# Four-layer graph network: setup rows for the second half made in groups 2 to 4, and a new static order

## The chip, the core and the metric

The kernel runs on one core of a Trainium2 chip. The metric is the device time of one execution in microseconds; the time before is the median of three runs, and the change is judged by the median time of the changed kernel. One of the three runs before (4820.43 us) stands apart from the other two and takes no part in the reasoning.

## The reference

The input is x, 128 graphs of 64 nodes with 512 features in float32, and an adjacency matrix of 64x64 per graph. Four layers follow each other. Each takes `h = relu(layernorm(x))` and adds its result to x.

```
layer 0:  h1 = relu(D^-1 H B^-1 H^T (h W1^T) + b1);  y = D^-1 H B^-1 H^T (LN(h1) W2^T) + b2;  x += y + h
layer 1:  A = exp(lrelu(8 tanh((s_i + s_j)/8))) * adj, s = (h w) a;  x += rownorm(A) * rowsum(adj) @ h @ w
layer 2:  x += rownorm(adj * exp(q k^T)) @ v,  q, k, v linear in h
layer 3:  T = rownorm(adj * exp(lrelu(sj_j + si_i + ab)));  x += relu(sum over k = 0..2 of T^k h Wk[k] + bk[k])
          sj, si: products of (h Wv + bv) with the two halves of a vector aw
```

Three small quantities that depend on weights alone matter for the change. `gb` is Wk^T bq, needed by the logits of layer 2. `c3` is Wv times each half of aw, two rows of 512, and `kap` is the sum of bv with both halves of aw, plus ab; all of these are needed by layer 3.

## The kernel before

The 128 graphs are taken as 16 groups of four tiles of 128 rows, two graphs to a tile. A first half runs layers 0 and 1 over the groups and stores x to a scratch tensor `xm`. A second half loads it again and runs layers 2 and 3. The weights of the halves share memory, so the halves are apart. Every large product is written as seven half-size products instead of eight (`strassen`, `chained`, and `product` in layer 3, where it is nested), which costs TensorE a little less and gives VectorE the sums and differences.

No loop sets the order in which instructions stand. The Python code records operations in a graph, each with an engine, an estimated cost and a priority, and `Graph.run` plays a list scheduler over that graph and writes out one fixed order for each engine: TensorE (PE), VectorE (DVE), ScalarE (ACT), GpSimd (POOL) and SyncE (SP). On SP stands every DMA. An engine takes its list strictly from the top, and SP does too: a DMA that waits for a buffer to come free holds up all DMAs behind it. The priority of an operation is a running number `G.prio` plus a shift from the table `AT`, set by `part(name)`. `PERIOD1` and `PERIOD2` space the groups of the two halves, and `STRETCH` scales the advance inside each layer. So a changed number in these tables can reorder everything.

Where the scheduler leaves TensorE a gap of over 1 us and a PSUM bank is free, `fill` puts matmuls of `ones` with `ones` in. They compute nothing that is used. Each such matmul has two records in the profile, as all float32 matmuls here.

Buffers are the other constraint. `tmp` has four slots of 128x512 floats; they take weight rows that are loaded for setup (`temp`) and, in layer 0, the planes of each `transposed` step, eight per group. `o` has two slots.

Setup code that comes ahead of group 0 is, in this order: `setup_l2` (Wq^T Wk, stored to a scratch tensor), the combinations of W1 and W2, `setup_l0`, `setup_l1`, the combinations of w, and then `setup_bq` and `setup_l3`:

- `setup_bq` loads four blocks of Wk, forms their sum weighted by bq in four DVE operations, multiplies by a column of ones on PE, and copies the result to `gb`.
- `setup_l3` loads ab, then for each half of aw: the half, bv, and four blocks of Wv, with five dot products on DVE (`dot`), and `spread`, which turns a column into a row over all partitions (one DVE product, one PE matmul, one ACT copy).

`setup_w3`, called under `part("wp")` for groups 1 and up, prepares the factors of the layer 3 weights during the first half; its loads are placed after the key `("z", g, k)`, which names the last operation of the normalisation between the two convolutions of layer 0 in that group. Such a key is for the scheduler alone: the semaphores of the built program follow from the memory that instructions touch.

In layer 3, `part("b0")` begins the long run of weight products of a group (L1124), whose weights are streamed from scratch tensors `fac`.

Of the kernel before, what the change touches and what calls it, by code (L numbers as in the profile page):

```python
# [14 lines left out]
P = 128  # L15
C = 64
D = 512
DH = 1024
T = 4
KD = D // P  # L20
# [151 lines left out]
def tile_adj_preln_d4(  # L172
# [6 lines left out]
    nc = tc.nc  # L179
    NG = adj.shape[0]  # L180
    G = Graph()
# [31 lines left out]
    def size(shape):  # L213
        n = 1
        for d in shape[1:]:
            n *= d
        return n

    for two in TWO:
        both = work.tile([P, max(sum(size(shape) * n for _, shape, n in tags) for tags in two)], F32,  # L220
                         name="_".join(tag for tags in two for tag, _, _ in tags))
        for tags in two:
            at = 0
            for tag, shape, n in tags:
                for i in range(n):
                    v = both[:, at:at + size(shape)]
                    at += size(shape)
                    if len(shape) == 3:
                        v = v.rearrange("p (a b) -> p a b", a=shape[1])
                    elif len(shape) == 4:  # L230
                        v = v.rearrange("p (a b c) -> p a b c", a=shape[1], b=shape[2])
# [23 lines left out]
    def c_mm(n, count):  # L255
        return 2 * count * max(n * 2 / 2400 + 0.0025, 0.111)
# [6 lines left out]
    def pe(cost, fn, r, w):  # L263
        return G.op("PE", cost, fn, r, w)

    def dve(cost, fn, r, w):
        return G.op("DVE", cost, fn, r, w)

    def dvp(cost, fn, r, w):
        return G.op("DVE", cost, fn, r, w, port=1)  # L270

    def act(cost, fn, r, w):
        return G.op("ACT", cost, fn, r, w)
# [7 lines left out]
    def dma(kb, fn, r, w, issue=0.34, lat=2.0):  # L281
        return G.op("SP", max(kb / 380.0, issue), fn, r, w, lat)

    def quad(b):
        return b.t.rearrange("p (c k) -> p c k", c=4)
# [1 line left out]
    FILL, LAT = 0.5, 2.3  # L287


    STRETCH, PERIOD1, PERIOD2 = (2.4057, 23.1237, 14.6194, 5.0478), 88.385, 152.83  # L290
    AT = {
        "x0": -4649.81, "apart": 515.41, "w1": 891.32, "b1": 147.15, "w2": 1055.04, "w": 146.66, "c1": 74.0, "l0":
        181.27, "c2": 131.25, "l1": 1241.14, "c": -4314.2, "g0": -2118.58, "g1": -4213.04, "g2": -574.45, "g3":
        -1827.82, "g": -443.79, "bq": -420.39, "l3": -143.58, "wg": 627.97, "wp": 228.79, "beg0": -1054.79, "beg1":
        -138.73, "end00": 1.09, "end01": -86.62, "end11": 256.44, "new2": -124.9, "new3": 81.75, "end2": -68.63,
        "end3": -133.99, "load1": -63.98, "load2": 661.26, "m": -63.44, "h0": 2.91, "p0": 25.16, "z0": -386.05,
        "q0": 47.65, "y0": -4107.25, "h1": -19.07, "p1": 5.7, "z1": -84.16, "q1": 20.96, "y1": -130.14, "s": -234.6,
        "t0": -462.0, "e0": -467.09, "t1": -348.17, "e1": -282.93, "hT": 524.3, "sh": 245.53, "lq": 730.58, "pt":
        -113.04, "v": 589.88, "pv": 1100.8, "s3": 672.72, "tt": 1008.78, "a0": 690.15, "b0": 538.95, "a1": 811.73,
        "ws": 2002.18, "load3": 441.07, "bk": 299.55,  # L300
    }

    def part(name):
        G.shift = AT[name]
# [28 lines left out]
        dma(8, lambda: nc.sync.dma_start(sb, src), [], [name])  # L333
        return sb

    def load_tmp(tag, n, shape_of, src):
        b = Buf(tag)
        dma(n * P * 4 / 1024, lambda: nc.sync.dma_start(shape_of(b.t), src), [], [b])
        return b

    def temp(src):

        return load_tmp("tmp", D, lambda t: t, src)

    xt, adjs, xmid, rows = {}, {}, {}, []

    def load_group(g, src, apart=0.0):
        b = Buf("adj")
        dma(500, lambda: nc.sync.dma_start(b.t, adj[g]), [], [b])
        adjs[g] = b  # L350
        for t in range(T):
            xx = Buf("x")
            at, key = src(g, t)
            G.shift += apart
            dma(300 if src is x_mid else 256, lambda xx=xx, at=at: nc.sync.dma_start(xx.t, at), key, [xx], lat=LAT if src is x_mid else 2.0)
            xt[g, t] = xx
# [27 lines left out]
    c3_b = const.tile([P, 2, D], F32, name="c3_b")  # L384
# [5 lines left out]
    def dot(in0, in1, acc, r, w):  # L390
        j = Buf("o")
        dvp(0.77, lambda: nc.vector.scalar_tensor_tensor(j.t, in0(), 1.0, in1(), op0=ALU.mult, op1=ALU.mult,
                                                         accum_out=acc()), r, [*w, j])
# [61 lines left out]
    def spread(col, dst, r, key):  # L455

        dg, p = Buf("tmp"), Buf("ps")
        dvp(0.75, lambda: nc.vector.tensor_mul(quad(dg), ident[:, None, :].to_broadcast([P, KD, P]),
                                               col()[:, :, None].to_broadcast([P, KD, P])), r, [dg])
        pe(c_mm(512, 1), lambda: nc.tensor.matmul(p.t, ones, dg.t, start=True, stop=True), [dg], [p])  # L460
        act(0.6, lambda: nc.scalar.copy(dst(), p.t), [p], [key])

    def setup_l1():
        wa, a_b = Buf("col"), temp(a.partition_broadcast(P))
        for c in range(KD):
            dot(lambda c=c: w_sb[:, c, :], lambda: a_b.t, lambda c=c: wa.t[:, c:c + 1], [(wm, c // 2), (wm, "given"), a_b], [(wa, c)])
        spread(lambda: wa.t, lambda: wa_b.t, [(wa, c) for c in range(KD)], wa_b)
# [15 lines left out]
            act(0.6, lambda c=c, e=e: nc.scalar.copy(e.t, ps[c].t), [ps[c]], [e])  # L483
            dma(256, lambda c=c, e=e: nc.sync.dma_start(wg_d[c * P:(c + 1) * P, :], e.t), [e], ["wg_d"])

    def setup_bq():

        pg, bk = Buf("ps"), Buf("o")
        for o in range(KD):
            k_ = temp(Wk[o * P:(o + 1) * P, :])  # L490
            if o == 0:
                dvp(0.45, lambda k_=k_: nc.vector.tensor_scalar(bk.t, k_.t, bq_c[:, 0:1], None, op0=ALU.mult), [k_, "bq_c"], [bk])
            else:
                dvp(0.85, lambda o=o, k_=k_: nc.vector.scalar_tensor_tensor(bk.t, k_.t, bq_c[:, o:o + 1], bk.t, op0=ALU.mult, op1=ALU.add),
                    [k_, "bq_c", bk], [bk])

        def mg():
            for c in range(KD):
                nc.tensor.matmul(pg.t[:, c:c + 1], bk.t[:, c * P:(c + 1) * P], ones[:, 0:1], start=True, stop=True)
        pe(c_mm(1, KD), mg, [bk], [pg])  # L500
        dve(0.2, lambda: nc.vector.tensor_copy(gb_c, pg.t[:, :KD]), [pg], ["gb"])

    def setup_l3():
        kk = Buf("mv")
        ab_t = load_tmp("rs", 1, lambda t: t, ab.partition_broadcast(P))
        for s in range(2):
            av, cc = temp(aw[s * D:(s + 1) * D].partition_broadcast(P)), Buf("col")
            bv_t = temp(bv3.partition_broadcast(P))
            dot(lambda bv_t=bv_t: bv_t.t, lambda av=av: av.t, lambda s=s: kk.t[:, s:s + 1], [bv_t, av], [(kk, s)])
            for c in range(KD):  # L510
                wv = temp(Wv3[c * P:(c + 1) * P, :])
                dot(lambda wv=wv: wv.t, lambda av=av: av.t, lambda c=c, cc=cc: cc.t[:, c:c + 1], [wv, av], [(cc, c)])
            spread(lambda cc=cc: cc.t, lambda s=s: c3_b[:, s, :], [(cc, c) for c in range(KD)], ("c3", s))
        dve(0.15, lambda: nc.vector.tensor_add(kap, kk.t[:, 0:1], kk.t[:, 1:2]), [(kk, 0), (kk, 1)], ["kap"])
        dve(0.15, lambda: nc.vector.tensor_add(kap, kap, ab_t.t), ["kap", ab_t], ["kap"])

# [492 lines left out]
    def layer3(g):  # L1009
# [9 lines left out]
        z = bcast_sum(lambda: ss[1].t, lambda: ss[0].t, [(ss[s], t) for t in range(T) for s in range(2)], extra=kap, on_pe=g == NG - 1)  # L1019
# [3 lines left out]
        dn, rn, tr, tt = Buf("col"), Buf("col"), Buf("bd"), Buf("tt")  # L1023
# [52 lines left out]


        part("b0")
        sx = Buf("sx")
        keys = lambda i, v: [(a3[2 * i + v], n) for n in range(3)]  # L1080
        block = lambda i, j: [(lambda v=v: a3[2 * i + v].t[:, :, 2 * j:2 * j + 2, :]) for v in range(2)]
# [47 lines left out]
        def snapshot(chain):  # L1129
            Z = Buf("zz")  # L1130
            for n, p in enumerate(banks[chain]):
                q = len(BLOCKS[n])
                act(q * P / 1200 + 0.17, lambda n=n, p=p, q=q: nc.scalar.copy(Z.t[:, 4 * n:4 * n + q], inner(p, q)), [p], [(Z, n)])
            return Z
# [46 lines left out]
        s3 = snapshot("X")  # L1181
# [31 lines left out]
    setup_l1()  # L1213
    part("c")
    W = combine(wm, w_sb, w_x, 2, D // 2, "DVE")
    part("bq")
    setup_bq()
    part("l3")
    setup_l3()
    for g in range(NG):  # L1220
        G.prio = g * PERIOD1
        if g:
            part("load1")
            load_group(g, x_in)
        for i, layer in ((0, layer0), (1, layer1)):
            stretch[0] = STRETCH[i]
            if g == 0:
                G.prio += AT["beg0" if i == 0 else "beg1"]
            if i == 0 and g == NG - 1:
                G.prio += AT["end00"]  # L1230
            if i == 1 and g >= NG - 2:
                G.prio += AT["end01" if g == NG - 2 else "end11"]
            layer(g)
        G.prio = g * PERIOD1
        part("wp")
        if g:
            for k in range(2):
                if 2 * g - 2 + k < 21:
                    setup_w3(2 * g - 2 + k, [("z", g - 1 + k, 1 - k)], [("z", g, k)])
# [10 lines left out]
    for k in range(1, 3):  # L1250
        b = Buf("h")
# [71 lines left out]
```

## Time and profile before

| | |
|---|---|
| runs | 2322.7, 2324.84 and 4820.43 us; median 2324.84 us |
| profiled execution, its own time | 2321.51 us |
| its span, first to last instruction | 2319.7 us |
| mean granted TensorE clock | 0.999 |
| PE, DVE, ACT, POOL busy | 2279.9, 1865.1, 1393.2, 1190.9 us |
| groups of the first half | one each 71.7 us |
| groups of the second half | one each 67.8 us |

A busy time is a sum over the whole span. What a saving is worth depends on the stage in which it falls: while PE has no idle time, an operation taken from DVE saves nothing. So the profile is read by stages: the start (until about 290 us), the even run of the first half, the passage between the halves (about 1130 to 1300 us), the second half, and the end.

### The profile page before, as it was taken

The numbers are of one execution on the slowest core, as the hardware profiler recorded it, in microseconds if no ns is written. First come the engines' busy times: TensorE is split into PE (matmuls) and PEld (weight loads), VectorE is DVE, ScalarE is ACT, GpSimd is POOL, SyncE is SP. The second block draws the span as 40 slices with busy tenths as digits, with TensorE's granted clock in tenths as the row PEclk, the third lists the DMA queues.
The fourth block names the chain that finished last, engine by engine and source line by source line (L and its number), as shares of the span: only waits on it lengthen the run. The fifth ranks groups of instructions, "written<-read, shape, count | busy, mean of one in ns | idle before, by whom it ended". The sixth has DMA issues, their size and how long they took to land.

```text
span 2319.7 us, 39752 instructions
## 1 busy us (share of the span) xinstructions
PE 2279.9 (98%) x14238; PEld 1866.4 (80%) x14238; DVE 1865.1 (80%) x4004; ACT 1393.2 (60%) x1993; POOL 1190.9 (51%) x1771
## 2 busy tenths in 40 slices
PE   8999999999999999999999999999999999999998
PEld 4676677776777767777688999999999989999898
DVE  7887877887778877787867888888888878788787
ACT  4766565675655765656657566566656655656542
POOL 7445556545665465543433455545455544545443
PEclk9999999999999999999999999999999999999999
DMA  6443233443333342323436877787787877878767
GB/s 232 103 104 77 78 98 79 102 90 79 83 91 94 90 90 58 74 71 68 97 98 161 223 222 229 234 223 213 226 244 213 235 215 217 222 224 225 200 200 242
DMA packets 403478, 355.12 MB, mean 153 GB/s; under 512 B 290896, under 2 KB 321872, under 8 KB 403280
## 3 DMA queue, kind: packets, MB, share of 16 engines
q1 hardware_dynamic: 403280, 352.58, 55.5%
q8 instruction: 112, 1.84, 0.3%
q14 instruction: 86, 0.70, 0.1%
HBM read 241.05 MB, written 44.33 MB: 123 GB/s over the span
## 4 chain that ended last, share of the span: by engine, by line
PE 84%; DMA 6%; DVE 5%; ACT 3%; issue 1%; POOL 1%; SPq 0%; DVEq 0%; ACTq 0%; POOLq 0%
PE ps L691 38%; PE ps L1124 19%; PE ps L930 15%; PE ps L592 4%; PE ps L844 2%; PE ps L1067 2%; DMA w2m_wm_a_wf<-fac 1%; DMA h<-o 1%; PE ps L999 1%; PE ps L961 1%; DMA x<-xm 1%; DMA z_hT<-tmp_mB_xi 1%; ACT h L583 1%; DVE st L562 1%; DMA tmp_mB_xi<-in_Wk_dram 0%
## 5 line engine op out<-in xcount | busy, mean ns | idle before, releaser
L583 ACT ACTIVATE h<-x,nm,rs 128x512 f32<-128x512 f32 x384 | 306.2, 812 | 234.9 <-POOL nm L570 220.3
L564 POOL TENSOR_SCALAR rs<-mv 128x1 f32<-128x1 f32 x320 | 104.6, 327 | 388.4 <-DVE mv L563 371.1
L1124 PE MATMUL ps<-w2m_wm_a_wf 128*128 128x128 f32 x2256 | 295.5, 277 | 3.8 <-DMA w2m_wm_a_wf<-fac 2.2
L1124 PEld LDWEIGHTS ps<-w2m_wm_a_wf 128*128 128x128 f32 x2256 | 275.8, 192 | 11.1 <-issue 4.0
L691 PE MATMUL ps<-w2m_wm_a_wf,s_s_zz 128*128 128x256 f32 x1152 | 274.8, 380 | 1.8 <-DVE s_s_zz L683 1.8
L1124 PE MATMUL ps<-w2m_wm_a_wf,tmp_mB_xi 128*128 128x128 f32 x1968 | 260.4, 277 | 9.8 <-DMA w2m_wm_a_wf<-fac 5.2
L1124 PEld LDWEIGHTS ps<-w2m_wm_a_wf,tmp_mB_xi 128*128 128x128 f32 x1968 | 243.2, 193 | 16.6 <-ACT h L583 7.5
L691 PEld LDWEIGHTS ps<-w2m_wm_a_wf,s_s_zz 128*128 128x128 f32 x1152 | 217.7, 190 | 39.7 <-issue 9.6
L691 PE MATMUL ps<-w2m_wm_a_wf,rT_vu_tt 128*128 128x256 f32 x1024 | 237.5, 380 | 2.0 <-ACT row_sh L453 0.7
L691 PE MATMUL ps<-wa_mem,mT_sx 128*128 128x512 f32 x512 | 238.1, 593 | 1.3 <-DMA wa_mem<-in_W1T_dram 1.0
L691 PEld LDWEIGHTS ps<-w2m_wm_a_wf,rT_vu_tt 128*128 128x128 f32 x1024 | 193.6, 190 | 48.5 <-issue 18.4
L565 POOL TENSOR_TENSOR rs<-rs,mhalf 128x1 f32<-128x1 f32 x320 | 209.2, 654 | 26.5
L562 DVE BATCH_NORM_STATS2 st<-x 128x6 f32<-128x512 f32 x256 | 176.1, 688 | 33.0 <-DMA x<-xm 25.7
L570 POOL TENSOR_SCALAR nm<-mv,rs 128x1 f32<-128x1 f32 x320 | 171.4, 537 | 30.2
L691 PE MATMUL ps<-wa_mem,s_s_zz 128*128 128x512 f32 x384 | 180.3, 593 | 0.0
L691 PEld LDWEIGHTS ps<-wa_mem,mT_sx 128*128 128x128 f32 x512 | 96.0, 191 | 103.9 <-issue 97.9
L818 ACT ACTIVATE z_hT<-z_hT 128x512 f32<-128x512 f32 x128 | 79.3, 630 | 133.6 <-DVE z_hT L711 133.6
L603 ACT COPY rT_vu_tt<-z_hT 128x1024 uint16<-128x1024 uint16 x128 | 146.7, 1162 | 16.6 <-DMA z_hT<-tmp_mB_xi 16.5
L719 POOL TENSOR_TENSOR u<-u,row_sh 128x256 f32<-128x256 f32 x96 | 75.4, 794 | 157.3 <-DVE u L661 134.7
L592 PEld LDWEIGHTS ps<-bd,h 128*128 128x128 f32 x1024 | 126.6, 192 | 36.4 <-issue 27.6
L885 POOL TENSOR_TENSOR x<-x,u 128x256 f32<-128x256 f32 x96 | 88.8, 950 | 113.0 <-DVE u L663 113.0
L601 ACT COPY o<-h 128x1024 uint16<-128x1024 uint16 x128 | 133.8, 1047 | 9.3 <-DVE h L1056 6.9
(205 smaller groups left out, 4991.8 us busy)
## 6 DMA issues: line engine op xcount, KB each, us to landing
w2m_wm_a_wf<-fac SPq DMA_DIRECT2D x110, 768.0 KB, 5.0
w2m_wm_a_wf<-fac SPq DMA_DIRECT2D x109, 576.0 KB, 4.8
x<-xm SPq DMA_DIRECT2D x128, 256.0 KB, 3.5
x<-in_x_dram SPq DMA_DIRECT2D x64, 256.0 KB, 2.8
xm<-x SPq DMA_DIRECT2D x64, 256.0 KB, 2.0
out_dram<-x SPq DMA_DIRECT2D x64, 256.0 KB, 3.9
adj<-in_adj_dram SPq DMA_DIRECT2D x32, 256.0 KB, 4.6
fac<-wp_bv_bk SPq DMA_DIRECT2D x63, 128.0 KB, 2.0
```

The lines of the kernel that those rows point to most:

```text
L562: dve(0.69, lambda i=i: nc.vector.bn_stats(st.t[:, i, :], src(i)), [r[i]], [(st, i)])
L564: small(0.28, lambda: nc.gpsimd.tensor_scalar_add(rs.t, mv.t[:, 1:2], EPS), [mv], [rs])
L565: small(0.62, lambda: nc.gpsimd.tensor_tensor(rs.t, rs.t, mhalf, ALU.pow), [rs], [rs])
L570: small(0.32, lambda: nc.gpsimd.tensor_scalar(nm.t, mv.t[:, 0:1], rs.t, -1.0, op0=ALU.mult, op1=ALU.mult), [mv, rs], [nm])
L583: act(0.82, lambda: nc.scalar.activation(h.t, xx.t, AF.Relu, bias=nm.t, scale=rs.t), [xx, nm, rs], [h])
L592: nc.tensor.matmul(quad(p)[:, c, :], h.t[:, c * P:(c + 1) * P], rhs(), start=True, stop=True)
L601: act(1.05, lambda: nc.scalar.copy(u16(planes.t).rearrange("p (q c) -> p q c", q=2), u16(src()).rearrange("p (c q) -> p q c", q=2)), ksrc, ...
L603: act(1.16, lambda: nc.scalar.copy(u16(dst()).rearrange("p c (k q) -> p c k q", q=2), u16(back()).rearrange("p (q c r) -> p c r q", q=2, c ...
L691: nc.tensor.matmul(p.t[:, :n], lhs()[:, c, :], rhs(c), start=first and c == 0, stop=c == kc - 1, skip_group_check=True)
L885: pool(0.78, lambda: nc.gpsimd.tensor_add(xx.t[:, cols], xx.t[:, cols], U.t[:, iu]), [xx, u], [xx])
L930: nc.tensor.matmul(pair(p.t)[:, o, :], a, b, start=first and o == 0 and c == 0, stop=c == 1, skip_group_check=True)
L1124: nc.tensor.matmul(inner(p, q)[:, r, :], at()[:, k, :], wv()[:, r, k, :], start=first and r == 0 and k == 0, stop=k == 2, skip_group_check ...
```

## The change

The two setups are no longer recorded ahead of group 0. `setup_bq` is recorded in group 2, and `setup_l3` is cut into its two halves, recorded in groups 3 and 4, all after layers 0 and 1 of the group. Their loads are now placed after the key `("z", g, 0)` of that group (the argument `r` of `load_tmp` and `temp`, through `when`). `sums` carries the column of sums and ab from the first half to the second. The number and kind of operations stay the same. In layer 3 of the last two groups the priority is raised by a new number, `late3` or `last3`, at the start of the weight products, which puts them later. And all numbers of `STRETCH`, `PERIOD1`, `PERIOD2` and `AT` are new, so the order of all engines is a new one.

```diff
-    STRETCH, PERIOD1, PERIOD2 = (2.4057, 23.1237, 14.6194, 5.0478), 88.385, 152.83
+    STRETCH, PERIOD1, PERIOD2 = (2.471, 24.4862, 14.5686, 4.3237), 83.899, 155.522
...
-        "x0": -4649.81, "apart": 515.41, "w1": 891.32, "b1": 147.15, "w2": 1055.04, "w": 146.66, "c1": 74.0, "l0":
...
+        "x0": -62.74, "apart": -18.5, "w1": -4.8, "b1": 731.14, "w2": 1137.04, "w": 220.06, "c1": -145.45, "l0":
...
+        "ws": 2232.24, "load3": 1252.28, "bk": -543.01, "late3": 743.67, "last3": 828.93,
...
-    def load_tmp(tag, n, shape_of, src):
+    def load_tmp(tag, n, shape_of, src, r=()):
         b = Buf(tag)
-        dma(n * P * 4 / 1024, lambda: nc.sync.dma_start(shape_of(b.t), src), [], [b])
+        dma(n * P * 4 / 1024, lambda: nc.sync.dma_start(shape_of(b.t), src), r, [b])
         return b
...
-    def setup_bq():
+    def setup_bq(when):
...
-            k_ = temp(Wk[o * P:(o + 1) * P, :])
+            k_ = temp(Wk[o * P:(o + 1) * P, :], when)
...
-    def setup_l3():
-        kk = Buf("mv")
-        ab_t = load_tmp("rs", 1, lambda t: t, ab.partition_broadcast(P))
-        for s in range(2):
-            av, cc = temp(aw[s * D:(s + 1) * D].partition_broadcast(P)), Buf("col")
-            bv_t = temp(bv3.partition_broadcast(P))
...
+    def setup_l3(s, when):
+        if not s:
+            sums.append((Buf("mv"), load_tmp("rs", 1, lambda t: t, ab.partition_broadcast(P), when)))
+        kk, ab_t = sums[0]
+        av, cc = temp(aw[s * D:(s + 1) * D].partition_broadcast(P), when), Buf("col")
+        bv_t = temp(bv3.partition_broadcast(P), when)
...
         part("b0")
+        if g >= NG - 2:
+            G.prio += AT["late3" if g == NG - 2 else "last3"]
...
-    part("bq")
-    setup_bq()
-    part("l3")
-    setup_l3()
+    sums = []
...
         part("wp")
+        if g in (2, 3, 4):
+            part("bq" if g == 2 else "l3")
+            when = [("z", g, 0)]
+            setup_bq(when) if g == 2 else setup_l3(g - 3, when)
+            part("wp")
```

## Prediction

> **What bounds the kernel now.** I read the busy times first, then a table by stretches, then PE's timeline where the table shows PE idle, then the list of waits.
>
> ```profile
> PE 2279.9 (98%) x14238; PEld 1866.4 (80%) x14238; DVE 1865.1 (80%) x4004; ACT 1393.2 (60%) x1993; POOL 1190.9 (51%) x1771
> ...
> 0.00:40.00 40.00, 33.11 (x131) 19.08 (x132) 24.87 (x65) 18.06 (x28) 24.73 (x47) 1.00 0.87 302
> 40.00:100.00 60.00, 57.82 (x218) 33.85 (x216) 53.43 (x94) 38.88 (x55) 34.81 (x36) 1.00 0.47 118
> 100.00:150.00 50.00, 47.64 (x208) 35.28 (x209) 44.80 (x99) 34.85 (x47) 21.57 (x39) 1.00 0.31 66
> ...
> 300.00:1100.00 800.00, 799.67 (x3482) 578.45 (x3481) 636.05 (x1406) 493.00 (x687) 437.53 (x679) 1.00 0.34 82
> 1100.00:1300.00 200.00, 195.68 (x1179) 163.98 (x1178) 155.31 (x333) 126.93 (x180) 85.39 (x146) 1.00 0.53 135
> ...
> 1850.00:2221.00 371.00, 362.48 (x3003) 336.03 (x3002) 294.28 (x627) 219.06 (x325) 183.65 (x254) 1.00 0.77 213
> 2221.00:2320.00 99.00, 87.33 (x814) 83.11 (x812) 80.53 (x159) 34.04 (x53) 40.15 (x51) 0.99 0.73 237
> ```
>
> The columns of the rows with a colon are the stretch, its length, the busy time and count of PE, its weight loads, DVE, ACT and POOL, the clock, the DMA share and GB/s. TensorE is the bound almost everywhere: from 300 to 1100 us it is idle for 0.3 us in 800. Idle time stands at both ends and between the halves: 11.4 us up to 150 us, 4.3 from 1100 to 1300, 8.5 from 1850 to 2221, 11.7 after that; with 4 us spread over the rest it is 40.
>
> The idle time is not all that is lost. Fill matmuls (L1199) count as busy, 138 records, 20.1 us. And a record's length overlaps the next, so I price PE work by start to start: 12 records of 128x512 from 38.04 to 43.19 us give 0.43 us each, eight of 128x256 from 86.73 to 88.45 give 0.215, eighteen of 128x128 from 2299.86 to 2301.88 give 0.112, 64 of the half-height L1067 in 3.84 us give 0.06. With 1064, 4736, 5728 and 1024 records of these kinds and about 55 us for 1536 narrow ones, the useful work is 457 + 1019 + 640 + 62 + 55 = about 2235 us. So 85 us of the span of 2319.7 do nothing useful. Counting the instructions ahead of certain points in PE's written order with the same prices, and reading the time of those points off the timeline, this loss stands at 14 us when the first product with W1 starts (30.69), 28 at the end of group 1 (285.86), 34 at the last L844 (1182), 40 at 1258, 61 at 2163, 67 at 2221 and 85 at the end. A third of it is made in the first 290 us.
>
> **A rule of the skill.** The Trainium skill, "Perfetto Trace Analysis", section "Identifying the Most-Contended Engine", says that the share of time in which matmuls are busy is a poor measure of how close TensorE is to its limit. Here it would leave 40 us to be won (2% of 2319.7), and the count of work leaves 85; the row of 300 to 1100 us shows the same from the other side, PE 800 of 800 and weight loads 578. The forecast goes by the count. "TensorE: Matmul & The Clock Gate", section "Wait — 56ns, not 53.3ns?", gives 215.7 ns from start to start for 512 columns on a warm clock; this float32 trace has 430 ns for a record of 512, so the trace's own spacing is used.
>
> **The start, where most of the change is.** Two things are in the way of PE before 150 us.
>
> ```profile
> 11.09 1.02 SPq L321 DMA_DIRECT2D w2m_wm_a_wf<-in_w_dram  x2
> 18.14 0.34 SPq L338 DMA_DIRECT2D tmp_mB_xi<-in_Wq_dram  x1
> ...
> 20.90 1.00 SPq L321 DMA_DIRECT2D wa_mem<-in_W1T_dram  x2
> ...
> 30.69 3.67 PE L691 MATMUL ps<-wa_mem,mT_sx 128*128 128x512 f32 x8 [0.98 <-DMA wa_mem<-in_W1T_dram]
> ...
> 139.55 1.73 PE L1199 MATMUL ps<-ones 128*128 128x128 f32 x14
> 141.20 1.98 PE L844 MATMUL ps<-y_qT,bd 128*128 128x512 f32 x4
> 143.02 2.17 PE L1199 MATMUL ps<-ones 128*128 128x128 f32 x18
> 146.90 1.27 PE L592 MATMUL ps<-bd,h 128*128 128x128 f32 x9 [1.71 <-DVE bd L873]
> ...
> L392 DVE SCALAR_TENSOR_TENSOR o<-tmp_mB_xi 128x512 f32<-128x512 f32 x10 | 8.7, 874 | 0.3 <-DMA tmp_mB_xi<-in_Wv_dram 0.2
> ```
>
> First, SP's queue stood from 12.1 to 18.1 us before a load into a tmp slot, with W1 behind it, and W1 was issued at 20.9 and used at 30.7. Second, DVE is 98.2 of 110 us busy between 40 and 150 us, and the largest gap ends with a DVE product (bd, L873).
>
> In the new order SP issues four blocks of Wq and Wk, four of x and one adj, 2.3 MB, and then W1, 2.1 MB. No full tmp slot lies ahead of it. At the 270 to 335 GB/s of the first two stretches of 20 us these 4.5 MB have landed 13.5 to 16.5 us after the first one starts at about 1.5 us: 15 to 18. Meanwhile PE does eight matmuls of Wq and Wk (16 x 0.43 = 6.9 us, from about 5 us on, when the first pairs have landed, by the 3.6 to 3.9 us that such loads took), L790 (0.6) and two L592 groups (1.8). The chain of stats, hypergraph matrix, h, L592 and copy is some 9 us of DVE, POOL and ACT work after x lands near 8 us. So the first product with W1 starts at about 18 us with 9.3 us of useful work done: loss 8.7 instead of 13.8. That is 5 us.
>
> The moved work is the second gain. Off DVE in the first 100 us go 10 dots (8.7 us), 10 accumulator reads (0.8), four weighted sums (0.5 + 3.1), two spread products (1.4) and small ones (0.4): 14.9 us, which takes DVE from 98 to 83 of 110 us, about the 80% at which PE had no idle time from 300 us on. What that can return is bounded by the gaps after 31 us: 13.8 us up to the end of group 1. Those at 97.9 (2.7 us with fill) and 139.6 (5.6) were 22 fill pairs, 0.38 us of gap to a pair. The new order has 16 pairs between the first product with W1 and the end of group 1, the old one 26, so gaps of 6 us remain where 10 were written. I take 3 us, with 0 and 9 as ends: W2 still arrives behind some 10.5 MB, near 35 us, and is then scaled on ACT and summed on POOL as before. Start in sum: -8, between 0 and -14.
>
> **Groups 2 to 4, where the work goes.** The matmuls (two of 128x512 and eight of one column, under 3 us) move from one PE-bound place to another: nothing. DVE gets 4 us in group 2 and some 5.5 each in groups 3 and 4; with 79.5% of 71.7 us busy it has 14.7 free in each, and PE's 0.3 us of idle time in 800 says that it isn't waited for. ACT gets two copies of 0.6, ACT is 62% busy. The cover is DVE's slack: without it, 15 us would come back whole. SP gets 16 loads of 256 KB and one small (4.2 MB against 82 GB/s of traffic, 34% DMA share). Each holds SP for 0.33 to 0.43 us, 6 us in three groups; but a load into tmp also waits for a slot, and behind it in SP's queue stand layer 0's transposes, whose data PE needs. The new key `("z", g, 0)` only tells the scheduler where to place them; the waits written at these loads are for tmp's earlier users (PE, DVE) and other DMAs. The longest such wait in the trace was the 6 us above, at the start, where all slots were full. I take 0, and 6 as the far end. A gain is excluded here, as PE has nothing to give.
>
> **Between the halves.** There are 21 fill pairs in the old order and 20 in the new. 0, with plus or minus 4.
>
> **The second half.** Each group is one of 67.8 us against 67.0 of work. The new `ws` and `load3` numbers move loads of fac and x, and the waits for those are small and irregular: fac 7.8 us in 8 waits, x 2.7 in one (2166.78). A new order redraws them. 0, from -8 to +10.
>
> **The end.** The work is the same; the overlap of the last two groups is not. In the old order 42 us of PE work stand between the last PV product of group 15 (L999, ending 2228.9) and the product L1046 of its transition (2270.8), and hide the chain of statistics, dots, bcast_sum and transposes on DVE. In the new order L1067 of group 14 stands ahead of that, and 22.7 us of useful work are left. That chain alone is: last scaling 1.0, stats 0.9, three POOL steps 1.5, h 0.8, dots 1.5, L746 and its matmul 1.5, and from 2264.59 to 2270.73 6.1, so 13 us. DVE has other work between (six differences of 0.56, four of L1091 at 1.0, sums), some 9 us. 22 against 22.7 just fits. The fill pairs say the same: 20 at the end instead of 13, so 7 x 0.38 = 3 us more. I take +3, from -3 to +19 (the 42 us not shortened).
>
> **Sum.** -8 + 0 + 0 + 0 + 3 = -5 us against the profiled execution's own 2321.51 us (span 2319.7 and 1.8 around it): 2316.5. The two close runs lie 1 and 3 us above that execution, so for the median I say 2318, 0.3% below 2324.84. About 2% is what a measurement of this kernel tells from no change.
>
> **The rivals.** (A) W2 and its chain end the start. What speaks for it: W2's place in the byte count stays, and ten fill pairs stand around L452 (bw2). Against: 14.9 us less on DVE. The gain of 8 shrinks to 1 and the end costs 3: 2325. (B) Slower: the chain of group 15 isn't shortened, since DVE is busy 80.5 of 99 us there and takes its list in order. PE then waits 42 - 22.7 = 19 us at the transition instead of 3. It decides from 11 us on: -8 + 19 = +11, 2334. For it: DVE is at 9 tenths from 2220 to 2300. Against: the differences that filled DVE there are off the chain, and fewer of them stand in between. (C) Much slower: in the second half, where DMA is 75 to 83% busy, each group waits for fac by 3 us where it waited by 0.5 on average; 16 x 2.5 = 40, with (B)'s end +11: 2374. Against it: old waits were 1.7 at most. (D) Waits of the second half shrink from 8.5 us idle to 2 and the end costs nothing: 2308. (E) That the moved setup doesn't leave the start: the written order has it between layer 0 and 1 products of later groups, so only its worth (3 us: 2321) is in doubt.
>
> **How the numbers follow.** Forecast 0.44, A 0.22, B 0.16, D 0.11, C 0.05, other 0.02. The range from 2299 to 2343 holds the forecast with its own ends, A, B and D, and leaves out C and half of the far ends. Faster by over 2% means under 2278 us: 43 of the 85 lost us would have to go, 0.02. Slower by over 2% means over 2371: C and a part of the rest, 0.05. Within 2%: 0.93.
>
> **What would show it.** First product with W1 at 17 to 20 us instead of 30.7; PE idle time up to 150 us 4 to 8 us instead of 11.4, and DVE 83 us busy between 40 and 150. The L844 of group 1 at 278 us instead of 286. No PE idle time of over 1 us in groups 2 to 5; if there is, and it ends with a transpose (L601 to L603), the loads blocked SP. A gap of 1 to 5 us before L1046 of the last group; over 10 means B. If the start is as long as before with W1 early, A holds. If the time is under 2300 or over 2343, the second half was moved, which I price at 0.

## The result, and the profile after

The changed kernel takes 2336.56 us (median of 7 runs, 2330.55 to 2342.23), the kernel before 2321.94 us beside it (median of 6; the run of 4820.43 us is left out): a ratio of 1.0063, with a 95% interval from 1.0047 to 1.008. It is slower by 0.6%, within 2%, where I had forecast 0.3% faster. The profiled execution took 2338.71 us, with a span of 2336.6 us, 16.9 us over the span before.

These are rows of the page and of the table by stretches, with the columns as before.

```profile
PE 2281.0 (98%) x14226; PEld 1863.7 (80%) x14226; DVE 1856.3 (79%) x4004; ACT 1390.3 (60%) x1993; POOL 1220.1 (52%) x1771
...
0.00:40.00 40.00, 34.20 (x122) 18.46 (x123) 27.84 (x59) 15.61 (x25) 24.23 (x37) 1.00 0.80 289
40.00:100.00 60.00, 57.76 (x246) 37.48 (x245) 52.81 (x101) 51.05 (x72) 42.02 (x53) 1.00 0.34 78
100.00:150.00 50.00, 50.00 (x213) 36.95 (x213) 39.82 (x92) 30.83 (x42) 21.57 (x35) 1.00 0.32 78
...
1300.00:1850.00 550.00, 533.83 (x4435) 494.50 (x4433) 435.38 (x928) 324.29 (x479) 279.48 (x379) 0.99 0.76 218
1850.00:2221.00 371.00, 359.87 (x2971) 334.11 (x2970) 291.29 (x628) 219.21 (x322) 195.95 (x261) 1.00 0.77 219
2221.00:2337.00 116.00, 102.18 (x944) 96.56 (x943) 88.20 (x177) 39.86 (x63) 43.58 (x54) 0.98 0.66 207
```

The middle of the second half, which the forecast had not shown, is this row in the profile before:

```profile
1300.00:1850.00 550.00, 547.07 (x4554) 507.55 (x4553) 456.73 (x962) 333.55 (x490) 283.17 (x396) 1.00 0.79 225
```

PE lacks 13.2 us of busy time there (547.07 against 533.83), and 119 records. The start, on the other hand, is better: idle time up to 150 us is 8.0 us (40 - 34.20, 60 - 57.76, 0) instead of 11.4.

The forecast's measure, loss (time less the priced work that stands ahead in PE's order), puts each microsecond in its place. The forecast calls the product at 285.86 us the end of group 1; it is the first y product (L844) of group 3, as these products come once a group, first at 93.64, 141.20, 217.61 and 285.86 us. In the changed kernel the loads of the moved setups go out from 155 us on (`setup_bq`), from 234 (first half of `setup_l3`) and from 309 (second half), so two thirds of the moved work fall in the first row and the rest in the second.

| stretch | loss added before | after | difference | forecast |
|---|---|---|---|---|
| to the product at 285.86 (after, the same at 281.05) | 27.5 | 19.3 | -8.2 | -8 |
| on to the product at 404.27 (after, 399.3) | 2.2 | 5.4 | +3.2 | 0 |
| on to the last y product of the first half | 4.0 | 4.2 | +0.2 | 0 |
| on to the first L1046 (after: L1048) | 6.4 | 5.9 | -0.5 | 0 |
| on to the 14th of these | 21.0 | 42.8 | +21.8 | 0 |
| on to the end | 23.4 | 23.8 | +0.4 | +3 |
| sum | 84.5 | 101.4 | +16.9 | -5 |

The second half spoils the forecast. The list of waits of PE from 1300 to 2221 us (what waited, for what, total, times, longest) is first that of the kernel before, then that of the changed one:

```profile
PE ps L1124 <- DMA w2m_wm_a_wf<-fac: 6.4, 6, 1.7
```

```profile
PE ps L1128 <- DMA w2m_wm_a_wf<-fac: 13.2, 8, 2.1
PE ps L1128 <- DVE w2m_wm_a_wf L1095: 5.3, 3, 2.1
PE ps L1128 <- DVE s_s_zz L1147: 2.6, 1, 2.6
PE ps L1128 <- ACT o L603: 2.1, 1, 2.1
```

Four releasers are named, but it is one place. In each of the 13 groups of this stretch PE stops for 1.2 to 2.6 us, always at the same run of weight products some 16 us after the group's L1048. From the second to the thirteenth group of the second half a group takes 70.43 us on average, where before it took 68.52: 11 x 1.91 = 21 us.

**Where the 1.9 us a group begin.** Two statistics meet after L1046 (L1048 after): that of layer 3's first tile, and that of the *next* group's first tile in layer 2. Each is two DVE steps and three small POOL steps (add L564, power L565, `nm` L570; after, L566, L567, L572), and only then can ACT make h. The timeline of the kernel before, in the group whose L1046 starts at 1397.68 (columns: start, length, engine, line, operation):

```profile
1401.15 0.23 POOL L564 TENSOR_SCALAR rs<-mv 128x1 f32<-128x1 f32 x1 [4.87 <-DVE mv L563]
...
1402.32 0.57 POOL L565 TENSOR_TENSOR rs<-rs,mhalf 128x1 f32<-128x1 f32 x1
1402.64 0.56 DVE L1104 TENSOR_TENSOR tmp_mB_xi<-w2m_wm_a_wf 128x384 f32<-128x384 f32 x1 [0.79 <-ACT w2m_wm_a_wf L1072]
1402.99 1.32 POOL L570 TENSOR_SCALAR nm<-mv,rs 128x1 f32<-128x1 f32 x2
1403.36 0.81 ACT L583 ACTIVATE h<-x,nm,rs 128x512 f32<-128x512 f32 x1 [0.76 <-POOL nm L570]
1405.28 1.24 SPq L602 DMA_TRANSPOSE h<-o  x1
```

And of the changed kernel, in the group whose L1048 starts at 1461.25:

```profile
1465.34 0.23 POOL L566 TENSOR_SCALAR rs<-mv 128x1 f32<-128x1 f32 x1 [5.60 <-DVE mv L565]
...
1466.21 0.56 DVE L1108 TENSOR_TENSOR tmp_mB_xi<-w2m_wm_a_wf 128x384 f32<-128x384 f32 x1 [0.17 <-ACT w2m_wm_a_wf L1074]
1466.31 0.58 POOL L572 TENSOR_SCALAR nm<-mv,rs 128x1 f32<-128x1 f32 x1
...
1466.98 0.46 POOL L566 TENSOR_SCALAR rs<-mv 128x1 f32<-128x1 f32 x1
1467.52 0.73 POOL L567 TENSOR_TENSOR rs<-rs,mhalf 128x1 f32<-128x1 f32 x1
1468.35 1.05 POOL L572 TENSOR_SCALAR nm<-mv,rs 128x1 f32<-128x1 f32 x1
1469.44 0.81 ACT L585 ACTIVATE h<-x,nm,rs 128x512 f32<-128x512 f32 x1 [3.26 <-POOL nm L572]
...
1471.35 1.57 SPq L604 DMA_TRANSPOSE h<-o  x1
1472.08 0.69 DVE L392 SCALAR_TENSOR_TENSOR o<-h,c_b 128x512 f32<-128x512 f32 x1 [2.72 <-ACT h L585]
...
1473.01 1.47 SPq L1120 DMA_DIRECT2D w2m_wm_a_wf<-fac  x3
1474.07 0.69 DVE L564 BATCH_NORM_STATS2 st<-x 128x6 f32<-128x512 f32 x1 [1.29 <-DMA x<-xm]
...
1477.70 1.63 PE L1128 MATMUL ps<-w2m_wm_a_wf,tmp_mB_xi 128*128 128x128 f32 x7 [2.06 <-DVE w2m_wm_a_wf L1095]
```

Counted from L1046 or L1048, DVE begins the sums of the product operands (L1104, L1108) at 4.96 us in both. Before, the first two steps of layer 2's tile begin ahead of that (at 4.33 and 4.64 us), and its `nm`, at 5.31, stands ahead of layer 3's `nm`; h is there at 5.7 us. (In the next group of the same kernel the power step begins at 4.97 us, beside the first sum, and takes 0.97 us instead of 0.57; there h comes at 7.1.) After, the first POOL step of all comes 0.6 us later (4.1 against 3.5), because DVE was late with the rows of V (L986, behind a second block transpose L1038); and layer 3's `nm` stands ahead. So all three steps of layer 2's tile fall beside DVE's sums, where they take 0.46, 0.73 and 1.05 us; and h comes at 8.2. Behind that h hang the transpose on SP, the loads of factors behind it (the first at 11.8 us here and at 11.4 in most groups, instead of 8.9), DVE's dot L392, and ACT's copies L1074. DVE stands 2.72 us for h and 1.29 us for the next x tile, so its differences L1095 and the factors come late together.

The theory ("late h" in the expectations): it is this h that makes the second half slower. The rivals: the moved rows disturb something that lasts, DMA transfers are late by themselves, or one queue behind h (SP's or DVE's) is the whole of it.

### The profile page after: what moved, and what is told of

It reads as the page before. It is cut to its first block, busy times and chain, and to the rows that moved or that the text cites. A ratio compares the mean times of both kernels' runs of the same rounds, so it can differ in the third digit from the quotient of the medians.

```text
span 2336.6 us, 39741 instructions
## 1 busy us (share of the span) xinstructions
PE 2281.0 (98%) x14226; PEld 1863.7 (80%) x14226; DVE 1856.3 (79%) x4004; ACT 1390.3 (60%) x1993; POOL 1220.1 (52%) x1771
## 4 chain that ended last, share of the span: by engine, by line
PE 77%; DVE 8%; DMA 6%; ACT 4%; POOL 3%; issue 2%; SPq 0%; POOLq 0%; DVEq 0%; ACTq 0%
PE ps L693 38%; PE ps L1128 17%; PE ps L932 11%; PE ps L594 5%; PE ps L846 2%; DVE rT_vu_tt L1038 2%; PE ps L1001 1%; DMA rw<-row 1%; ACT h L585 1%; DMA h<-o 1%; POOL nm L572 1%; DMA w2m_wm_a_wf<-fac 1%; POOL rs L567 1%; DVE bd L971 1%; DVE st L564 1%
## 5 line engine op out<-in xcount | busy, mean ns | idle before, releaser
L566 POOL TENSOR_SCALAR rs<-mv 128x1 f32<-128x1 f32 x320 | 110.9, 346 | 392.5 <-DVE mv L565 370.5
L1128 PE MATMUL ps<-w2m_wm_a_wf,tmp_mB_xi 128*128 128x128 f32 x1968 | 261.3, 277 | 26.2 <-DMA w2m_wm_a_wf<-fac 13.2
L567 POOL TENSOR_TENSOR rs<-rs,mhalf 128x1 f32<-128x1 f32 x320 | 212.0, 662 | 26.1
L564 DVE BATCH_NORM_STATS2 st<-x 128x6 f32<-128x512 f32 x256 | 175.5, 686 | 37.1 <-DMA x<-xm 24.3
L572 POOL TENSOR_SCALAR nm<-mv,rs 128x1 f32<-128x1 f32 x320 | 175.4, 548 | 31.2
L605 ACT COPY rT_vu_tt<-z_hT 128x1024 uint16<-128x1024 uint16 x128 | 147.3, 1161 | 28.1 <-DMA z_hT<-tmp_mB_xi 27.5
L603 ACT COPY o<-h 128x1024 uint16<-128x1024 uint16 x128 | 133.8, 1046 | 36.0 <-DVE h L1058 32.1
L594 PEld LDWEIGHTS ps<-bd,h 128*128 128x128 f32 x1024 | 127.5, 192 | 32.5 <-issue 21.9
L984 POOL TENSOR_TENSOR u<-u,wp_bv_bk 128x512 f32<-128x512 f32 x48 | 64.2, 1337 | 157.2 <-ACT u L636 157.2
```

The source lines that it names most:

```text
L564: dve(0.69, lambda i=i: nc.vector.bn_stats(st.t[:, i, :], src(i)), [r[i]], [(st, i)])
L566: small(0.28, lambda: nc.gpsimd.tensor_scalar_add(rs.t, mv.t[:, 1:2], EPS), [mv], [rs])
L567: small(0.62, lambda: nc.gpsimd.tensor_tensor(rs.t, rs.t, mhalf, ALU.pow), [rs], [rs])
L572: small(0.32, lambda: nc.gpsimd.tensor_scalar(nm.t, mv.t[:, 0:1], rs.t, -1.0, op0=ALU.mult, op1=ALU.mult), [mv, rs], [nm])
L594: nc.tensor.matmul(quad(p)[:, c, :], h.t[:, c * P:(c + 1) * P], rhs(), start=True, stop=True)
L603: act(1.05, lambda: nc.scalar.copy(u16(planes.t).rearrange("p (q c) -> p q c", q=2), u16(src()).rearrange("p (c q) -> p q c", q=2)), ksrc, ...
```

## The experiments

The ratios are to the kernel before in the same set of runs (2321.6 to 2322.9 us in all sets). h is the median time from L1046 (L1048) to the start of that h over 12 groups, the period the mean of 11 group lengths.

| kernel | h, us | period, us | time, us | ratio to before, 95% |
|---|---|---|---|---|
| `layer2_first_dve` | 5.0 | 68.04 | 2309.89 | 0.9943 (0.993 to 0.9957) |
| `layer2_first` | 5.6 | 68.18 | 2311.99 | 0.9957 (0.9944 to 0.9971) |
| `both_orders` | 5.7 | 67.94 | 2309.07 | 0.9949 (0.9932 to 0.9966) |
| `both_no_late` | 5.7 | 68.18 | 2314.7 | 0.9962 (0.9949 to 0.9976) |
| before | 5.7 and 7.1 or later in turn | 68.52 | 2322 | 1 |
| `move_only` | 5.7 and 7.1, irregular | 68.62 | 2325.67 | 1.0012 (1.0003 to 1.002) |
| `late_h_before` | 7.1 | 68.78 | 2322.04 | 0.9998 (0.9989 to 1.0007) |
| `pool_order` | 7.2 | 68.83 | 2320.24 | 0.9995 (0.9985 to 1.0005) |
| `dve_order` | 7.1 | 68.93 | 2319.19 | 0.9988 (0.998 to 0.9996) |
| `second_half_numbers` | 8.2 | 69.89 | 2343.26 | 1.0083 (1.0068 to 1.0098) |
| changed | 8.2 | 70.43 | 2336.56 | 1.0063 (1.0047 to 1.008) |
| `fac_first` | 8.2 | 71.10 | 2343.73 | 1.0103 (1.0084 to 1.0121) |

Eight of these move steps in an engine's written list after the scheduler has made it: `put(o, at)` takes operation o to place `at` in the order, as long as no operation in between depends on it or uses its buffers. Nothing else changes there, save the two numbers of both_no_late. Of the code only the lines that move something are shown; `marks` holds the operations of a kind in the order in which they were recorded.

**pool_order: one POOL step moved in the changed kernel.** Layer 3's `nm` of the first tile goes behind the next group's `nm` of layer 2.

```diff
+        for a, b in zip(self.marks["nm3"][0::4], self.marks["nm2"][4::4]):
+            if seqs.index(a) < seqs.index(b):
+                put(a, seqs.index(b) + 1)
```

> The changed kernel with one step moved in POOL's list: in each group of the second half the last small step (nm) of layer 3's first tile goes behind the three small steps of the next group's first layer 2 tile, as in the kernel before. Theory (late h): in the changed kernel that tile's h is 8.2 us after the group's L1048 instead of 5.7, because its POOL steps start behind that nm and then run beside DVE's sums of the product operands; SP holds the load of the next factors behind the transpose of that h, and TensorE waits 1.2 to 2.6 us a group. Then h comes at about 6.5 us, the factors load at about 9.8 instead of 11.4, the wait of about 16 us after L1048 falls under 0.5 us, and the time falls by 12 to 18 us, to 2319 to 2325. Rival (transfers): the factors come late because of DMA traffic, not of their issue: the wait stays and the time stays within 4 us of 2336.6. Rival (moved rows): the second half is slower for another reason that starts in the first half: no change.

h came at 7.2 us, not 6.5, the load at 10.4, the wait shrank to 0.8 to 1.4 us in seven of the twelve groups and was under 0.5 us in the others, and the time fell by 16 us. One step of POOL, 0.3 us of work, is worth 16 us.

**dve_order: one DVE step moved in the changed kernel.** The second block transpose of layer 3 goes directly behind the first.

```diff
+        for a, b in zip(self.marks["tt"][0::2], self.marks["tt"][1::2]):
+            put(b, seqs.index(a) + 1)
```

> The changed kernel with one step moved in DVE's list: the second block transpose of layer 3 (L1038) goes in front of the masking product of layer 2 (L971), as in the kernel before, so that the rows of V (L986) come about 1.1 us earlier. Theory (late h): the statistics behind it on DVE come 0.6 us earlier and finish more of POOL's small steps ahead of DVE's sums of the product operands; h comes at about 7 us instead of 8.2, the wait shrinks to about a half, the time falls by 6 to 14 us, to 2323 to 2331. Rival (transfers, or moved rows): within 4 us of 2336.6.

h at 7.1 us, time down by 17 us, a little more than expected. Two edits on two engines give the same h and the same period (68.83 and 68.93).

**both_orders: the two edits together.**

> Both moves together: POOL's and DVE's local order around the start of layer 3 as in the kernel before, everything else of the changed kernel as it is. Theory (late h): h at 5.7 us after L1048 in nearly all groups, factors issued at 8.9 us, no wait left there; groups of the second half 68.5 us instead of 70.4, and the time 2315 to 2321: what I predicted, with the gain of the start showing. Rival (moved rows, transfers): the time stays above 2330.

h came at 5.7 us in ten of twelve groups, as in the better groups of the kernel before, and the time was 2309.07 us, 6 us better than the lower end of what I expected, and faster than both kernels. In the list of waits from 1300 to 2221 us little is left of the factors (first row), and DVE's waits for h and for the next x tile are 0.22 and 0.23 us (the other rows, from the timeline) where they were 2.72 and 1.29:

```profile
PE ps L1145 <- DMA w2m_wm_a_wf<-fac: 1.0, 4, 0.4
```

```profile
1467.54 0.69 DVE L407 SCALAR_TENSOR_TENSOR o<-h,c_b 128x512 f32<-128x512 f32 x1 [0.22 <-ACT h L601]
...
1468.46 0.69 DVE L579 BATCH_NORM_STATS2 st<-x 128x6 f32<-128x512 f32 x1 [0.23 <-DMA x<-xm]
```

The moved rows, the new numbers (save for what these two entries restore) and the DMA traffic are all still there, so none of them makes the second half slow by itself. The gain over my forecast comes from the second half, which lost 13.1 us up to the 14th L1048 instead of 21.0 before: the kernel before had half of its groups at 7.1 us.

**fac_first: SP's list alone changed.** Of the three loads of factors behind the transpose of h (`tr`), the first goes ahead of it and of the second x load.

```diff
+        fac = set(self.marks["fac"])
+        for tr in self.marks["tr2"][4::4]:
+            sp = [o for o in seqs if o.eng == "SP"]
+            i = sp.index(tr)
+            n = 0
+            while sp[i + 1 + n] in fac:
+                n += 1
+            for m in range(n, 0, -1):
+                put(tr, seqs.index(sp[i + m]) + 1)
+                put(sp[i - 1], seqs.index(tr))
```

> The changed kernel with SP's list changed alone: the load of the factors that TensorE waits for (L1120, first of the three) goes in front of the load of the next group's second x tile and of the transpose that waits for h. POOL, DVE and ACT keep the order of the changed kernel, so h stays late. Theory (late h, by way of SP's queue): the wait goes as far as this load alone made it; DVE's differences, which stand behind the same h (L392), may take over a part. Time down by 10 to 18 us, to 2319 to 2327. Rival (DVE's list): the wait is ended by DVE's differences L1095 behind h, and the load is only the releaser that the profile names: gap stays over 1 us and ends with DVE, time within 4 us of 2336.6. Rival (transfers): the load is issued earlier and lands no earlier.

The theory's number was missed, in the wrong direction: 7 us slower than the changed kernel. The load was issued at 8.4 us, and the waits for factors fell from 13.2 to 2.0 us, but a little further on PE stopped for a bank that DVE had not read (L1171 is this kernel's line for L1147), first row. The other rows, from the timeline, tell why DVE was late: it stood 2.73 us for the late h, as in the changed kernel, and then 2.60 us for the next x tile, where the changed kernel has 1.29.

```profile
PE ps L1023 <- DVE s_s_zz L1171: 21.7, 13, 3.3
```

```profile
1331.68 0.69 DVE L412 SCALAR_TENSOR_TENSOR o<-h,c_b 128x512 f32<-128x512 f32 x1 [2.73 <-ACT h L606]
...
1334.98 0.69 DVE L584 BATCH_NORM_STATS2 st<-x 128x6 f32<-128x512 f32 x1 [2.60 <-DMA x<-xm]
```

The load of that x tile can start only when ACT has made the late h out of the buffer that it overwrites. It goes out 9.0 us after L1048 in both kernels, but here behind 576 KB of factors. So the experiment settles less than it should: it adds some 1.3 us of delay of its own. What it does show is that DVE stands for the same h, so that relieving SP's load of factors alone leaves DVE's wait; that the gap ends with DVE is what the rival (DVE's list) had said. That the factors named at the gap are not the cause is shown by pool_order and dve_order, which leave SP's list as it is.

**move_only: the moved setup with all numbers of the kernel before.** The numbers are those of the kernel before, `late3` and `last3` are 0, and the setups are recorded in groups 2 to 4.

> The kernel before with the two setups moved to groups 2 to 4 and all numbers as they were before, late3 and last3 zero. The start of SP's list is then that of the kernel before without the loads that moved; W1 is not issued earlier. The order around layer 3 is that of the kernel before. My prediction has 3 us for what leaves DVE in the first 100 us and 0 for the work in groups 2 to 4: 2318 to 2320 beside a before of 2321.6. If the moved rows cost in groups 2 to 4 (the changed kernel lost some 3 us more there than before): 2321 to 2324. If the moved rows are to blame for the slow second half: above 2330.

2325.67 us, 0.12% above before and a little above my 2321 to 2324. The period of the second half is that of before (68.62), so the moved rows don't slow it. By 111 us this kernel had lost 15.8 us where the one before had lost 20.8 at 120.6: 5 us gained. By the product at 285.86 (here 289.32) that gain was gone (27.5 in both), and by the end of the first half it had lost 8.5 us more than the kernel before, most of it (6 to 7 us) in groups 5 to 15, where none of the moved work stands. The move alone is no gain, even at the start.

**second_half_numbers: only the numbers of the second half changed.** Nothing is moved; the second half's entries of the tables, `late3` and `last3` are the new ones.

> The kernel before with nothing moved, and of the new numbers only those of the second half (STRETCH of layers 2 and 3, PERIOD2, the shifts of the second half, late3 and last3). Its local order around layer 3 is that of the changed kernel: on POOL the step nm of layer 3's tile ahead of the next group's three, on DVE the second block transpose behind the masking product. Theory (late h): h at 8.2 us after L1046 in every group, period 70.4 us, and the time is that of before plus some 20 us for the second half and 1 to 3 for the end: 2341 to 2346. Rival (moved rows): as before, 2321.

2343.26 us, as expected: h at 8.2 us in all groups, period 69.89. The cause lies in the new numbers of the second half and not in the rows that moved.

**late_h_before: the two steps put the other way round in the kernel before.**

`nm` goes directly behind its power step, and the block transpose behind the masking product.

```diff
+        for a, b in zip(self.marks["nm3"][0::4], self.marks["pw3"][0::4]):
+            put(a, seqs.index(b) + 1)
+        for a, b in zip(self.marks["tt"][1::2], self.marks["pt"][3::2]):
+            put(a, seqs.index(b) + 1) if seqs.index(b) > seqs.index(a) else None
```

> The kernel before with no number changed and nothing moved, but with the two steps of the lists put as in the changed kernel: on POOL the nm of layer 3's first tile ahead of the next group's three small steps, on DVE the second block transpose of layer 3 behind the masking product. Theory (late h): h goes from 5.7 and 7.1 in turn to 8.2 us after L1046, the wait after the first weight products appears in each group, the period goes from 68.5 to about 70.4 us and the time rises by 15 to 25 us, to 2337 to 2347. Rival: these two steps cost in the changed kernel only in company with its other new orders: within 4 us of 2321.6.

A miss of mine: 2322.04 us, no difference. The period rose only from 68.52 to 68.78. The trace shows that h did not become as late as I had expected: 7.1 us in nearly all groups and not 8.2, since the move on DVE cost nothing there. In that kernel DVE has waited for PE at this point (0.72 us before the rows of V), so the transpose behind the masking product fits in. By h, the period is where the table puts it. The move of the DVE step is thus late only in company with the changed kernel's other new order around it: these two entries alone don't make the loss.

**both_no_late: both orders restored, `late3` and `last3` zero.**

> The version with both orders restored (2309.1 us), and late3 and last3 zero, so that the weight products of the last two groups are no longer put later. My prediction priced the new overlap of the end at +3 us, the rival (B) at +19. If late3 and last3 made the end worse, this is 1 to 5 us faster than 2309.1; if they hide the chain of the last group as they should, it is up to 10 us slower.

2314.7 us, 5.6 above both_orders; the two intervals overlap, so this is not told apart for certain. From the 14th L1048 to the end it lost 24.1 us, both_orders 21.9. The new shifts of the last two groups are worth about 2 us in these traces; they are not what made the kernel slower.

**layer2_first and layer2_first_dve: an order that neither kernel has.**

All five steps of the next group's first layer 2 statistic go ahead of layer 3's.

```diff
+        for a, b in zip(self.marks["s3"], self.marks["s2"][1:]):
+            for o in b:
+                put(o, seqs.index(a[0])) if seqs.index(o) > seqs.index(a[0]) else None
```

> The changed kernel with the two statistics that meet after L1048 exchanged: the first tile of the next group's layer 2 goes ahead of layer 3's first tile, on DVE (two steps) and on POOL (three steps). This is the order of neither kernel, and the late rows of V on DVE stay as they are in the changed kernel. Theory (late h): what counts is only when that h is ready, not that an order of before is restored; its POOL steps are done at about 5.5 us, ahead of most of DVE's sums, h comes at 5.6 to 6.2 us, the period falls from 70.4 to 67.9 to 68.4 us and the time to 2309 to 2317. Rival (the order of before matters otherwise, as by the second statistic that is now late): above 2325.

> The same exchange, and DVE's second block transpose ahead of the masking product as in both_orders. Theory (late h): h at about 4.9 us, the earliest that ACT's four copies of layer 3 let it be; if the gain goes on below 5.7 us, the period falls under 67.9 us and the time under 2309; if 5.7 us is early enough, because the factors then wait for nothing, it is the same as both_orders within 3 us (2306 to 2312).

Both came out as the theory says. With an order that is not that of before, h at 5.6 us gives 68.18 us a group and 2311.99 us. With dve_order's edit on top, h is at 5.0 us and nothing more is gained (2309.89 against 2309.07 for both_orders): 5.7 us is early enough.

The theory stands. Over twelve kernels the period follows the time of this one h: about 68 us up to 5.7, 68.8 at 7.1, and 70 to 71 at 8.2. It is not the whole of the period: at the same 8.2 us second_half_numbers has 69.89 and fac_first 71.10. How the loss is shared between SP's queue and DVE's, which both stand behind this h, is not shown, and which of the new numbers makes the order so was not tried.

## Why the prediction was wrong, point by point

**The start: right in its sum, not in its way there.** -8 forecast, -8.2 measured. W1 went out at 5.76 us, and its first product started at 19.50, in the 17 to 20 that I gave:

```profile
5.76 1.06 SPq L321 DMA_DIRECT2D wa_mem<-in_W1T_dram  x2
```

```profile
19.50 1.93 PE L693 MATMUL ps<-wa_mem,mT_sx 128*128 128x512 f32 x4
```

The loss at that product is 10.2 us (19.5 - 9.3), against 13.8: 3.6 us where I said 5. But none of that lasts. At group 0's first y product (93.64 us before, 90.78 after) both kernels have lost about 18 us. Ahead of the product of bw2 (L452) alone, where rival A had it stop, PE of the changed kernel does no useful work for 3.4 us (fill matmuls from 57.91, then idle):

```profile
57.91 2.05 PE L1203 MATMUL ps<-ones 128*128 128x128 f32 x16
...
61.33 1.12 PE L452 MATMUL ps<-o,ones 128*128 128x512 f32 x2 [1.37 <-POOL o L449]
```

The whole -8.2 comes between there and the product at 285.86 us: the kernel before loses some 10 us more on that way, the changed kernel under 2. For this part I had said 3. So it is luck that the sum fits. I gave as the reason that 14.9 us leave DVE, but DVE's busy time from 40 to 150 us is 92.6 us, not 83, as layer work that now comes earlier took the place; and move_only, which takes the same work off DVE, kept no gain. The move alone thus doesn't bring the 8.2 us. Whether the new order of the start would bring them without the move, or only with it, no run shows.

**Groups 2 to 4: 0 forecast, 3.2 measured** from 281 to 399 us, inside my far end of 6. Of the moved work only the second half of `setup_l3` lies there; the other two thirds stand before it, in a stretch (131 to 281 us) that lost under 2 us. I had said that a gap of over 1 us would contradict the step; there are two, at 301.62 (1.39 us) and 341.96. At the second, the timeline tells the order of things:

```profile
335.25 2.04 SPq L550 DMA_DIRECT2D fac<-wp_bv_bk  x2
337.40 1.24 SPq L604 DMA_TRANSPOSE z_hT<-tmp_mB_xi  x1
...
340.48 1.16 ACT L605 COPY rT_vu_tt<-z_hT 128x1024 uint16<-128x1024 uint16 x1 [0.40 <-DMA z_hT<-tmp_mB_xi]
341.96 1.35 PE L693 MATMUL ps<-w2m_wm_a_wf,rT_vu_tt 128*128 128x256 f32 x5 [1.89 <-ACT u L661]
```

The transpose's source was written at 335.15 (the end of ACT's L603, which began at 334.12), but SP stood at two stores of factors until 337.3. ACT's list stood at the copy L605 for that transpose, and the copy L661 for which PE waits comes behind it. That a transpose held on SP would be the price was my far end; but I had it held by a load into `tmp`, and here it is a store of `setup_w3`, whose place is also new. How much of the 3.2 us is the moved work's and how much the new order's, these runs don't separate.

**Between the halves and the rest of the first half: right** (-0.5 and +0.2).

**The second half: the step that failed.** I wrote "A new order redraws them. 0, from -8 to +10", and it was +21.8. I took each wait for factors as an accident of its own, since before they were few and irregular, and summed them as if they would be redrawn at random. But a group repeats the same order 16 times, so a wait that gets into the order is paid in each group: 1.9 us here are 21 over 11 groups. And most of the waits of before were no accident: of the six for factors in the list above, four stand some 15 to 16 us behind an L1046 whose h came at 7.2 us or later. I also had the size of this stage too low. A group took 67.8 us by my figure; from the first L1046 to the 14th the mean is 68.5, and my own losses (40 us at 1258, 61 at 2163) say that 21 us were lost there.

The place could have been found before any run. The two entries stand in the written order of the changed kernel: on POOL `nm` between the two triples, on DVE the transpose behind the masking product. The size could not be read off the lists: in the kernel before the same two entries cost nothing (late_h_before). I compared PE's order closely and the other engines' only at the start.

Rival C named the sign and the symptom, a wait for factors in each group, at 2.5 us a group for 16 groups; 1.9 was measured. But its mechanism, crowded DMA, was wrong: both_orders moves more bytes per second there (227 GB/s against 218) and doesn't wait.

**The end: +3 forecast, +0.4 measured.** The wait before the last group's L1048 was 1.0 us after a run of fill matmuls, in my 1 to 5; B needed over 10.

```profile
2280.26 1.95 PE L1203 MATMUL ps<-ones 128*128 128x128 f32 x16
2283.22 0.69 PE L1048 MATMUL ps<-rT_vu_tt,bd 128*64 128x64 f32 x16 [1.01 <-DVE rT_vu_tt L1038]
```

## What to carry to other kernels

Where a static order repeats per group, compare the lists of *all* engines in one period before and after a change, and price a difference times the number of periods. What one difference costs has to be measured, as the same one can be free in another order. Look for the small steps from which several in-order queues hang at once (here three POOL steps of 128x1, with SP, ACT and DVE behind them); the releaser that the profile names at the gap is the last of several to arrive, and relieving it alone may help nothing. And give a re-drawn order a range as wide as one such step times the periods.

## What was not expected of the hardware

The small POOL steps are longer beside DVE's operations on two operands. From 1300 to 2221 us of the changed kernel `nm` took 0.27 us in each of the 14 cases where no such DVE operation (tensor-tensor or scalar-tensor-tensor, without a PSUM operand) ran beside it, and 0.58 to 1.29 us, median 1.05, in the 90 where one did; the power step took 0.57 us in all 16 cases without and 0.57 to 1.35, median 0.67, in the 88 with. The order alone changes it: in one group of layer2_first_dve the add, power and `nm` of layer 2 come ahead of the sums and take 0.23, 0.57 and 0.27 us, those of layer 3 behind them take 0.52, 0.85 and 0.55; in dve_order layer 3's come first, and take 0.23, 0.57 and 0.27. "SBUF — State Buffer" of the Trainium skill, section "Who interferes with whom", has a rule for that: a DVE instruction with two inputs in SBUF contends with a GpSimd instruction that reads SBUF, as its second input comes through the read interface that both share, and the order of issue decides which of the two blocks. The lengths agree with it; no run here took the sums away to test it by itself. It makes the cliff: three steps that begin 0.6 us later and behind one more end 2.5 us later.

After some of the gaps of 2 us and more, TensorE's granted clock fell to 0.50 for 3.41 us. The last `profile` row of the group at 1461.25 above shows PE going on at 1477.70 after a gap of 2.06 us; these rows of the table by stretches are what follows, that whole group, and a group without such a drop:

```profile
1477.92:1481.33 3.41, 3.41 (x18) 3.41 (x18) 1.57 (x3) 2.04 (x3) 1.56 (x3) 0.50 0.67 265
1461.25:1532.84 71.59, 69.40 (x566) 64.52 (x566) 55.69 (x120) 41.72 (x61) 36.59 (x49) 0.98 0.74 215
1532.84:1602.88 70.04, 68.04 (x566) 62.88 (x567) 55.94 (x120) 41.53 (x61) 36.75 (x49) 1.00 0.79 221
```

The 18 records in the drop take 0.19 us each, where records of 128x128 otherwise start 0.112 us apart. With the same number of records PE is busy in that group for 69.40 us instead of 68.04. Three groups of the eleven are like this (with gaps of 2.06, 2.6 and 2.13 us), so that some 4 of the 21 us lost are not idle time. Gaps of 2.09 us in another group and of 2.85 us in fac_first had no such drop behind them, so the length of the gap alone doesn't decide.
